# The mask of a context attention as a matmul, paced zero fills, and a planner's estimates

## The chip, the cores and the metric

The kernel runs on one core of a Trainium2 chip. The metric is the device time of one execution in microseconds (us). Times of single steps come from one profiled execution, whose span begins with the first instruction and ends with the last.

## The reference

A decoder of four layers on x of 8 x 256 tokens by 256 channels, with a context of 8 x 77 rows. Each layer has a self attention, a context attention and a feed-forward part, each followed by a residual add and a layer norm. The parts differ from layer to layer. Cut to the one that is edited, the context attention of L1 (16 heads of 64):

```python
q, k, v = heads(x @ Wq + bq), heads(ctx @ Wk + bk), heads(ctx @ Wv + bv)
scores = where(mask, -1e9, q @ k.T / 8)        # mask: 8 x 256 x 77, the same for all heads
x = layernorm(x + softmax(scores) @ v @ Wo + bo)
```

The context attention of L0 has the same sizes, without mask and biases. The feed-forward parts of L0, L1 and L2 route each token to two of 8, 8 and 14 experts.

## The kernel before, in words

**Order of the work.** The program is written batch by batch, and `Arrange` (L67 on) then reorders it. It builds the graph of all instructions, gives each an issue and a completion time (`cost`, L116 on: a formula by engine, kind and element count), adds a delay for a signal from one engine to another (`SIGNAL`, with 25 ns for pairs that are not listed), and simulates the engines. At each step an engine takes the earliest in program order among those that could start soon; it looks at most 300 instructions past the oldest one that is still open (`WINDOW`). The result is a fixed order for each of the five queues: TensorE, VectorE, ScalarE, GpSimd and SyncE, the last of which issues most DMAs. On the chip, each queue then runs strictly in that order, and an instruction that waits holds all that stand behind it on its queue. The estimates don't act on the chip; they only decide the order.

**Context attention** (`cross64`, L1308 on, for L0 and L1). Per batch of 256 tokens:
- `queries`: 8 blocks of Wq, two float32 matmuls each into PSUM, evicted to qT by VectorE and ScalarE in turn (for L1 with the bias, L570 and L572).
- `weights`: for both halves t of the tokens and both halves of the heads, 8 score matmuls (L1367) of 64 x 128 by 77 columns go into two PSUM tiles of 4 heads, 308 columns. Without a mask, VectorE takes the row maximum from PSUM (L1387) and subtracts it into P (L1388). With the mask, ScalarE first copies the scores to P in SBUF (L1380), VectorE overwrites the masked ones there with -8e9 (L1381, from mk, which SyncE loads as bytes), and maximum and subtraction then read P.
- `normed`: ScalarE takes the exponential (L1347), VectorE the sums z (L1349) and their reciprocals (L1350), and P is multiplied by them (L1351). For t = 0 it is one call of 1232 columns with the multiplication on GpSimd; for t = 1 two of 616, multiplied on GpSimd without a mask and on VectorE with it.
- `outputs`: P is transposed on TensorE (L1403), multiplied with V (L1418), and evicted to oT. Then come the output projection, the residual (GpSimd's xb, L697, then L702), and the norm: bn_stats and bn_aggr (L674, L676), an inverse root on GpSimd (L604, L605), the scaling (L685), a transpose of x (L657). Routing steps for the experts follow (L3038 to L3120), and GpSimd scatters the tokens to the experts' table l1x (L1486).

**Zero fills.** The experts' tables lie in HBM and are filled with zeros by SyncE from one SBUF tile `zero` of 128 x 256 (L1456 to L1474), which is set once in `setup` (L636). `slot_rows(kind)` issues one fill (mostly 1024 KB) per step; L0's attention makes three steps per turn of its loop for L0's and L1's tables (17 and 3 fills), and `l1_attn` (L1709 on) four per batch for L2's table, 30 fills in all. The scatter into a table waits for its fills.

**Handoff to L1's self attention.** After L0's experts, GpSimd gathers their results gy (L1530), and VectorE adds them to x (L3227), norms and hands them to the projections (L577).

Of the kernel before, what the change touches and what calls it, by code (L numbers as in the profile page):

```python
# [10 lines left out]
BF = mybir.dt.bfloat16  # L11
# [5 lines left out]
ALU = mybir.AluOpType  # L17
AX = mybir.AxisListType
# [3 lines left out]
P = 128  # L22
NB = 8
# [5 lines left out]
SC = 77  # L29
# [37 lines left out]
class Arrange:  # L67

    ENGINES = ("PE", "DVE", "Activation", "Pool", "SP")
    SIGNAL = {("DVE", "Pool"): 77, ("Activation", "Pool"): 69, ("PE", "Pool"): 100, ("DVE", "PE"): 44, ("Activation", "PE"): 43, ("Pool", "Pool"): 77}  # L70
    TABLES = [{f, "Identity", "Copy", "Square", "Relu", "Abs"} for f in ("Exp", "Ln", "Silu", "Gelu", "Gelu_apprx_tanh")]
    WINDOW, LOOK, RESERVE, SPAN = 300, 30, 2, 3413.0
    SLACK = {"PE": 100, "DVE": 150, "Activation": 200, "Pool": 200, "SP": 0}
# [42 lines left out]
    def cost(self, nd):  # L116
        i, e, kind = nd.ins, nd.e, nd.kind
        outs, ins = ([x for x in s if hasattr(x, "bass_ap")] for s in (i.outs, i.ins))
        n = max([self.count(x.ap) for x in (*outs, *ins)] or [1])
        ps = any(self.made.get(x.bass_ap.tensor.name, ("",))[0] == "ps" for x in (*outs, *ins))  # L120
        if kind == "InstMatmult":
            mv, w = ins[0], ins[1]
            n = self.count(outs[0].ap)
            wide = "float32" in str(w.dtype)
            turn = bool(i.is_transpose)
            own = n / 2.4 * (1 if not wide or turn else 4) + 3
            rows, cols = tuple(i.tile_size)
            part = 4 if 32 in (rows, cols) else 2 if 64 in (rows, cols) else 1
            low = 25 if not wide else 109 if turn else 223
            nd.pe = max(own, low), part, (rows, cols), tuple(i.tile_position), wide  # L130
            return None, nd.pe[0] + 178
        if kind == "InstDMACopy":
            on_chip = lambda x: self.made.get(x.bass_ap.tensor.name, ("dr",))[0] != "dr"
            nd.size = max([4 * self.count(x.ap) * list(x.ap)[0][1] for x in (*outs, *ins) if on_chip(x)] or [1 << 18])
            return (1250 if e == "Pool" else 60), 2000
        last = len(outs) > 1
        if e == "DVE":
            if kind in ("InstMax", "InstMaxIndex", "InstBNStatsAggregate"):
                n = 28
            elif kind == "InstReciprocal":  # L140
                n *= 5.6
            s = 65 + n / 0.96
            if n <= 256 and ps and kind == "InstTensorScalarPtr" or kind == "InstCopyPredicated":
                s += 60
            return s, s + 95
        if e == "Activation":
            if kind == "InstTensorCopy":
                s = 23 + 0.9 * n
                return s, s + 115
            s = 144 + 0.83 * n + (108 if last else 0) + (45 if not ps and 64 < n <= 512 else 0)  # L150
            return s, s + (40 if 500 < n < 600 else 105)
        if kind == "InstTensorTensor":
            s = 360 + 190 * n if n <= 8 else 145 + 2.13 * n
        elif kind == "InstMemset":
            s = 30 + 0.9 * n
        elif kind == "InstTensorCopy":
            s = 100 + 0.9 * n
        else:
            s = 240 + 0.85 * n
        return s, s + 50  # L160
# [309 lines left out]
class Build:  # L470
# [837 lines left out]
    def cross64(self, pre, bias, mask, row, route):  # L1308
        nc, a = self.nc, self.a
        with ExitStack() as ctx:  # L1310
# [9 lines left out]
                nc.sync.dma_start(kT, self.l0k[:, 6 * NC :].rearrange("p (n c) -> p n c", n=2))  # L1320
                self.l1wk = self.load_w(a["L1_xattn_Wk"], 2, 1024)
            keys = lambda n: kT[:, n, :] if bias else self.l0kT[n] if n < 6 else kT[:, n - 6, :]
            if mask is not None:
                big = self.t(w1, [P, 1], "big")
                nc.vector.memset(big, -8.0e9)
            def queries(b):

                qT = self.t(w2, [P, 8, S], "qT")
# [24 lines left out]
            def weights(b, qT):  # L1353

                Pt = []
                for t in range(2):
                    pr = self.t(w2, [P, H, SC], f"P{t}")
                    if mask is not None:
                        mk = self.t(w2, [P, SC], "mk", U8)
                        nc.sync.dma_start(mk, mask[b, t * P : (t + 1) * P, :])  # L1360
                    for hf in range(2):

                        two = [self.ps()[:, : 4 * SC].rearrange("p (h s) -> p h s", h=4) for par in range(2)]
                        for m in range(4):
                            for par in range(2):
                                r = slice(64 * par, 64 * par + 64)
                                nc.tensor.matmul(  # L1367
                                    two[par][:, m, :],
                                    qT[r, 4 * hf + m, t * P : (t + 1) * P],
                                    keys(4 * hf + m)[r, b * SC : (b + 1) * SC],  # L1370
                                    start=True,
                                    stop=True,
                                )
                        for par in range(2):
                            psv = two[par]
                            po = pr[:, 8 * hf + par : 8 * hf + 8 : 2, :]
                            mx = self.t(self.sm, [P, 4], "mx", bufs=8)
                            src = psv
                            if mask is not None:
                                nc.scalar.copy(po, psv)  # L1380
                                nc.vector.copy_predicated(  # L1381
                                    po,
                                    mk.unsqueeze(1).to_broadcast([P, 4, SC]),
                                    big.unsqueeze(1).to_broadcast([P, 4, SC]),
                                )
                                src = po
                            nc.vector.tensor_reduce(mx, src, AX.X, ALU.max)  # L1387
                            nc.vector.tensor_tensor(  # L1388
                                po, src, mx.unsqueeze(2).to_broadcast([P, 4, SC]), ALU.subtract
                            )  # L1390
# [44 lines left out]
            for b in range(NB):  # L1435
                oT = outputs(Pt, V, between)
                for _ in between:
                    pass
                if b + 1 < NB:
                    Pt = weights(b + 1, self.q_next)  # L1440
                    between = queries(b + 2) if b + 2 < NB else iter(())
                    if mask is not None:
                        for _ in range(3):
                            next(between, None)
                    V = values(b + 1)
                for t in range(2):
# [9 lines left out]
    def slot_rows(self, kind):  # L1456
# [4 lines left out]
        )[kind]  # L1461
        xg = self.t(self.dr, [n + spare, D], f"l{kind}x")
        eo = self.t(self.dr, [m, D], f"l{kind}e")
        zeroed = []
        self.slots[kind] = (xg, eo, zeroed)
        for t, first, end in ((xg, 0, n), (eo, (U0 * 256, m, U2 * 256)[kind], m)):
            for at in range(first, end, 8 * P):
                w = min(8, (end - at) // P)
                z = self.nc.sync.dma_start(
                    t[at : at + w * P, :].rearrange("(p r) c -> p r c", p=P), self.zero.unsqueeze(1).to_broadcast([P, w, D])  # L1470
                )
                if t is xg:
                    zeroed.append(z.ins)
                yield  # L1474
# [234 lines left out]
    def l1_attn(self):  # L1709
        nc, a = self.nc, self.a  # L1710
        with ExitStack() as ctx:
# [2 lines left out]
            Wqk = self.load_w(a["L1_attn_Wqk"], 2, 1024)  # L1714
            Wv = self.load_w(a["L1_attn_Wv"], 2, 256)
            Wp = self.load_w(a["L1_attn_Wp"], 2, 256)
            zeros = self.slot_rows(2)
            bk, bq = self.fm("l1_bk"), self.fm("l1_bq")
            mxps, vps = self.l1c
            rows = [slice(32 * j, 32 * j + 32) for j in range(4)]  # L1720
# [101 lines left out]
            for b in range(NB):  # L1822
# [4 lines left out]
                if b + 1 < NB:  # L1827
                    q, k, v = project_in(b + 1)
                    q2 = shift(b + 1, q, k)
                for _ in range(4):  # L1830
                    next(zeros, None)
                self.settle(1)
                weigh(*prev)
            for _ in zeros:
                pass
            self.settle()

    def heads_out(self, b, oT, W, row, pool, eps=None, route=None):
# [1612 lines left out]
```

## Time and profile before

| | |
|---|---|
| median of 3 runs | 3338.68 us (3325.26 to 3339.35) |
| the profiled execution, own time | 3340.12 us |
| its span | 3338.3 us |
| busy: TensorE, VectorE | 3038.5 us (91%), 1911.4 us (57%) |
| busy: ScalarE, GpSimd | 1080.6 us (32%), 921.4 us (28%) |
| L0's context attention | about 489 to 716 us |
| L1's self attention | about 1028 to 1335 us |
| L1's context attention | about 1334 to 1622 us |
| L1381, predicated copy x64 | 35.6 us of VectorE, 556 ns each |
| L1380, copy to SBUF x64 | 24.2 us of ScalarE |
| zero fills of L2's table | issued 1031 to 1122 us |

How to read it: PE is TensorE (PEld its weight loads), DVE VectorE, ACT ScalarE, POOL GpSimd, SP SyncE. In the slices, each digit is a fortieth of the span: the busy share in tenths, and for PEclk the clock that TensorE was granted. A group has line, engine, operation, output and inputs with their shapes, count, then busy us and mean ns of one, then the idle time just before it and what ended that. A wait has who waited, for whom, us in total, times, and the longest. A float32 matmul appears as two records.

### The profile page before, as it was taken

Reading aid. Unit: us, or ns where it says so; the run is one execution under the profiler, and the core shown is the slowest. Engines: PE = TensorE matmul, PEld = TensorE weight load, DVE = VectorE, ACT = ScalarE, POOL = GpSimd, SP = SyncE. Lnnn points to the kernel's source line nnn. Section 1 sums busy time; section 2 is a strip of 40 time slices with the busy share of each in tenths; the row PEclk is TensorE's granted clock in tenths of the full one; section 3 lists DMA queues with packets and bytes.
Section 4 is the critical chain, followed back from the end, with each engine's and each line's share of the span. In section 5 each row is a group of like instructions: output and inputs, shape, how many; then the busy total and the mean of one; then the engine's idle time right before and its main releaser. Section 6 shows DMA issues by size and latency. Waiting matters only on the chain. (4 is left out here: it accounts for less than half of the span.)

```text
span 3338.3 us, 49578 instructions
## 1 busy us (share of the span) xinstructions
PE 3038.5 (91%) x19222; PEld 2213.6 (66%) x19242; DVE 1911.4 (57%) x4814; ACT 1080.6 (32%) x2429; POOL 921.4 (28%) x1379
## 2 busy tenths in 40 slices
PE   5888779989998999899999999999898899888997
PEld 3445447758886777666555677666576588567876
DVE  6877677761003555888412132268688354699883
ACT  4666633222221223333211111145333111334441
POOL 2122253353322121223200000122244352633342
PEclk6888979999997999989999999999888899999998
DMA  4132020125547600002001133310000374200000
GB/s 161 50 100 95 26 88 25 31 84 177 186 174 249 228 14 1 23 22 78 26 4 53 42 127 129 110 44 14 1 14 26 127 234 155 83 13 4 7 7 10
DMA packets 136763, 254.04 MB, mean 76 GB/s; under 512 B 15075, under 2 KB 104939, under 8 KB 128843
## 3 DMA queue, kind: packets, MB, share of 16 engines
q1 hardware_dynamic: 112266, 150.80, 13.5%
q0 software_dynamic: 23104, 98.95, 8.7%
q8 instruction: 156, 2.56, 0.3%
q10 hardware_dynamic: 1152, 1.05, 0.1%
q14 instruction: 85, 0.69, 0.1%
HBM read 163.50 MB, written 87.26 MB: 75 GB/s over the span
## 5 line engine op out<-in xcount | busy, mean ns | idle before, releaser
L577 PE MATMUL ps<-xt,w 128*128 128x256 f32 (+1 forms) x1408 | 456.3, 471 | 3.4 <-issue 2.5
L577 PE MATMUL ps<-w,hT 128*128 128x256 f32 (+1 forms) x1792 | 399.4, 381 | 0.0
L577 PEld LDWEIGHTS ps<-w,hT 128*128 128x128 f32 (+1 forms) x1792 | 331.4, 187 | 57.4 <-issue 6.2
L577 PEld LDWEIGHTS ps<-xt,w 128*128 128x128 f32 x1408 | 266.1, 197 | 147.5 <-issue 121.3
L577 PE MATMUL ps<-gT,w 128*128 128x256 f32 (+1 forms) x1472 | 356.0, 399 | 7.3 <-ACT hT L1594 6.2
L577 PEld LDWEIGHTS ps<-gT,w 128*128 128x128 f32 x1472 | 275.1, 190 | 78.9 <-ACT hT L1594 9.7
L577 PE MATMUL ps<-w,oT 128*128 128x256 f32 x704 | 165.4, 389 | 1.0 <-ACT oT L565 0.5
L697 POOL TENSOR_TENSOR xb<-x,rows 128x256 f32<-128x256 f32 x80 | 60.0, 755 | 379.2 <-DVE res L702 379.0
L577 PEld LDWEIGHTS ps<-w,oT 128*128 128x128 f32 x704 | 133.4, 193 | 26.6 <-issue 3.8
L1594 ACT ACTIVATE hT<-ps,more 128x256 f32<-128x256 f32 x152 | 72.0, 475 | 206.2 <-PE ps L577 198.9
L1605 DVE COPY y<-ps 128x512 f32<-128x512 f32 x41 | 28.3, 691 | 172.2 <-PE ps L577 164.3
L1104 ACT ACTIVATE e<-ps,nm 128x128 bf16<-128x128 f32 (+1 forms) x256 | 104.0, 446 | 61.3 <-DVE nm L1099 60.9
L1670 DVE TENSOR_TENSOR hT<-hT,ps 128x512 f32<-128x512 f32 x56 | 38.4, 688 | 145.1 <-PE ps L577 144.2
L1403 PE MATMUL ps<-ident,P 128*77 128x128 f32 x512 | 90.8, 307 | 28.7 <-DVE P L1351 17.9
L1403 PEld LDWEIGHTS ps<-ident,P 128*77 128x77 f32 x512 | 66.6, 164 | 66.0 <-DVE P L1351 20.7
L1666 ACT ACTIVATE hT<-ps 128x512 f32<-128x512 f32 x56 | 33.3, 597 | 229.9 <-PE ps L577 229.9
L2029 DVE SCALAR_TENSOR_TENSOR f<-ps,f 128x512 f32<-128x512 f32 x128 | 80.4, 682 | 30.5 <-ACT f L2028 27.6
L1351 POOL TENSOR_TENSOR P<-P,z 128x1232 f32<-128x1232 f32 (+1 forms) x32 | 55.1, 1731 | 148.5 <-DVE z L1350 124.6
L2028 ACT ACTIVATE f<-ps,neg 128x512 f32<-128x512 f32 x128 | 78.2, 690 | 54.5 <-PE ps L2025 54.4
L1126 DVE TENSOR_REDUCE cm<-ps 128x2 f32<-128x512 f32 (+1 forms) x96 | 59.7, 684 | 53.6 <-PE ps L1067 53.3
L1418 PE MATMUL ps<-PT,V 77*64 77x256 f32 x512 | 85.1, 423 | 5.0 <-DVE PT L563 1.7
L1920 DVE TENSOR_TENSOR hT<-hT,ps 128x320 f32<-128x320 f32 x64 | 31.2, 488 | 98.3 <-PE ps L577 94.9
(669 smaller groups left out, 6467.7 us busy)
## 6 DMA issues: line engine op xcount, KB each, us to landing
l2x<-zero SPq DMA_DIRECT2D x28, 1024.0 KB
l0x<-zero SPq DMA_DIRECT2D x16, 1024.0 KB
w<-in_L_ffn_rg SPq DMA_DIRECT2D x8, 1024.0 KB
w<-in_L_ffn_ru SPq DMA_DIRECT2D x8, 1024.0 KB
w<-in_L_ffn_rd SPq DMA_DIRECT2D x8, 1024.0 KB
l2e<-y SPq DMA_DIRECT2D x22, 256.0 KB
l0e<-y SPq DMA_DIRECT2D x19, 256.0 KB
rows<-in_rows SPq DMA_DIRECT2D x7, 544.0 KB
```

What stands on the lines that cost most here:

```text
L577: self.nc.tensor.matmul(out, lhsT, rhs, start=(i == 0), stop=(i == last))
L697: self.nc.gpsimd.tensor_tensor(t, self.X[i], row, ALU.add)
L1104: nc.scalar.activation(e[:, : (t + 1) * P], ps[j][:, i, :], AF.Exp, bias=nm[:, t, h : h + 1], accum_out=z[:, t, h : h + 1],)
L1126: nc.vector.tensor_reduce(cm[:, at : at + len(gs)], ps[j], AX.X, ALU.max)
L1351: eng.tensor_tensor(pr, pr, z.unsqueeze(2).to_broadcast([P, n, SC]), ALU.mult)
L1403: nc.tensor.transpose(psv[:, m, t * P : (t + 1) * P], Pt[t][:, 2 * n + m, :], self.ident)
L1418: nc.tensor.matmul(po[64 * m : 64 * m + 64, :S], V[:, h * 64 : (h + 1) * 64], ahead[n % 2][:, m, :], start=True, stop=True,)
L1594: nc.scalar.activation(hT[:, f + m, :], ps[:, m * 256 : (m + 1) * 256], func, bias=more[:, f + m : f + m + 1])
L1666: nc.scalar.activation(hT[:, f, :], ps, func, **({"bias": bias(f)} if bias else {}))
L1670: nc.vector.tensor_tensor(hT[:, f, :], hT[:, f, :], ps, ALU.mult)
L2028: nc.scalar.activation(f[:, j], ps[j], AF.Exp, bias=neg1)
L2029: nc.vector.scalar_tensor_tensor(f[:, j], ps[j], 1.0, f[:, j], ALU.max, ALU.min)
```

## The change

1. L1's mask. GpSimd turns mk into `low` (bf16: -1e30 where masked, else 0). Before the score matmuls of a pair of PSUM tiles, TensorE multiplies the identity by `low`, repeated for four heads, into each tile, and the scores are accumulated on it. ScalarE's copy and VectorE's predicated copy go, and maximum and subtraction read PSUM.
2. Zero fills. Ahead of every second fill of L2's tables, and every third of L0's and L1's, GpSimd sets `zero` again. The memset has to wait until the fills before it have read the tile, and the next fills wait for the memset. `l1_attn` now makes two steps per batch (16), and `cross64` of L1 makes two per batch and all that are left after the last batch (14).
3. Estimates. A VectorE step that needs another VectorE step waits 50 ns instead of 25 after its completion; predicated copies and long scaled operations in SBUF (over 200 elements) complete 130 ns after issue time instead of 95; GpSimd copies 150 instead of 50; short GpSimd scalings (up to 64 elements) are estimated at 150 + 0.85 n instead of 240 + 0.85 n.

```diff
-    SIGNAL = {..., ("Pool", "Pool"): 77}
+    SIGNAL = {..., ("Pool", "Pool"): 77, ("DVE", "DVE"): 50}
...
+            if kind == "InstCopyPredicated" or kind == "InstTensorScalarPtr" and n > 200 and not ps:
+                return s, s + 130
             return s, s + 95
...
         elif kind == "InstTensorCopy":
             s = 100 + 0.9 * n
+            return s, s + 150
+        elif n <= 64 and kind == "InstTensorScalarPtr":
+            s = 150 + 0.85 * n
...
                         nc.sync.dma_start(mk, mask[b, t * P : (t + 1) * P, :])
+                        low = self.t(w2, [P, SC], "low", BF)
+                        nc.gpsimd.tensor_scalar(low, mk, -1.0e30, 0.0, ALU.mult, ALU.add)
                     for hf in range(2):
 
                         two = [self.ps()[:, : 4 * SC].rearrange("p (h s) -> p h s", h=4) for par in range(2)]
+                        if mask is not None:
+                            for par in range(2):
+                                nc.tensor.matmul(
+                                    two[par], self.identb, low.unsqueeze(1).to_broadcast([P, 4, SC]), start=True, stop=False
+                                )
...
-                                    start=True,
-                                    stop=True,
+                                    start=mask is None,
+                                    stop=mask is None or m == 3,
...
-                            src = psv
-                            if mask is not None:
-                                nc.scalar.copy(po, psv)
-                                nc.vector.copy_predicated(
...
-                                src = po
-                            nc.vector.tensor_reduce(mx, src, AX.X, ALU.max)
+                            nc.vector.tensor_reduce(mx, psv, AX.X, ALU.max)
                             nc.vector.tensor_tensor(
-                                po, src, mx.unsqueeze(2).to_broadcast([P, 4, SC]), ALU.subtract
+                                po, psv, mx.unsqueeze(2).to_broadcast([P, 4, SC]), ALU.subtract
                             )
...
+                if mask is not None:
+                    for _ in range(2 if b + 1 < NB else 30):
+                        next(self.zeros, None)
...
-        zeroed = []
+        zeroed, n_done, per = [], 0, 2 if kind == 2 else 3
...
                 w = min(8, (end - at) // P)
+                if n_done % per == 0:
+                    self.nc.gpsimd.memset(self.zero, 0.0)
+                n_done += 1
                 z = self.nc.sync.dma_start(
...
-                for _ in range(4):
-                    next(zeros, None)
+                for _ in range(2):
+                    next(self.zeros, None)
...
-            for _ in zeros:
-                pass
```

More of the change, by code (lines that the diff above doesn't have):

```diff
@@ L69 @@
     ENGINES = ("PE", "DVE", "Activation", "Pool", "SP")
-    SIGNAL = {("DVE", "Pool"): 77, ("Activation", "Pool"): 69, ("PE", "Pool"): 100, ("DVE", "PE"): 44, ("Activation", "PE"): 43, ("Pool", "Pool"): 77}
+    SIGNAL = {("DVE", "Pool"): 77, ("Activation", "Pool"): 69, ("PE", "Pool"): 100, ("DVE", "PE"): 44, ("Activation", "PE"): 43, ("Pool", "Pool"): 77, ("DVE", "DVE"): 50}
     TABLES = [{f, "Identity", "Copy", "Square", "Relu", "Abs"} for f in ("Exp", "Ln", "Silu", "Gelu", "Gelu_apprx_tanh")]
@@ L1322, in cross64 @@
             keys = lambda n: kT[:, n, :] if bias else self.l0kT[n] if n < 6 else kT[:, n - 6, :]
-            if mask is not None:
-                big = self.t(w1, [P, 1], "big")
-                nc.vector.memset(big, -8.0e9)
             def queries(b):
@@ L1377, in weights @@
                             mx = self.t(self.sm, [P, 4], "mx", bufs=8)
-                            src = psv
-                            if mask is not None:
-                                nc.scalar.copy(po, psv)
[L1381 to L1385, printed above, removed]
-                                src = po
-                            nc.vector.tensor_reduce(mx, src, AX.X, ALU.max)
+                            nc.vector.tensor_reduce(mx, psv, AX.X, ALU.max)
                             nc.vector.tensor_tensor(
-                                po, src, mx.unsqueeze(2).to_broadcast([P, 4, SC]), ALU.subtract
+                                po, psv, mx.unsqueeze(2).to_broadcast([P, 4, SC]), ALU.subtract
                             )
@@ L1716, in l1_attn @@
             Wp = self.load_w(a["L1_attn_Wp"], 2, 256)
-            zeros = self.slot_rows(2)
+            self.zeros = self.slot_rows(2)
             bk, bq = self.fm("l1_bk"), self.fm("l1_bq")
```

## The prediction, as put on record

> **What bounds the kernel now.** I read the page's slices first, then the same stretch of work in two stages, then the groups of VectorE in both, then the zero fills.
>
> ```profile
> PE   5888779989998999899999999999898899888997
> ...
> DVE  6877677761003555888412132268688354699883
> ...
> PEclk6888979999997999989999999999888899999998
> ```
>
> TensorE is busy nearly throughout, so most of the kernel is bound by it. One slice is 83.5 us. Slices 16 to 18 (1335 to 1585 us) are the L1 context attention: there VectorE stands at 8, beside 8 and 9 of TensorE. The same function runs for L0 in slices 6 and 7 without a mask. That gives a measured twin. I cut four batches out of each, from the z sum (L1349) of one batch to that of the fourth after it (busy us by engine, then granted clock, DMA share, GB/s):
>
> ```profile
> 549.36:663.24 113.88, 113.10 (x836) 88.17 (x835) 85.91 (x253) 33.48 (x68) 40.39 (x44) 1.00 0.09 31
> 1377.91:1517.36 139.45, 126.77 (x837) 96.77 (x836) 124.45 (x338) 49.94 (x116) 41.91 (x52) 0.91 0.08 25
> ```
>
> The matmul records are the same (836 and 837), yet L1 needs 139.45 us for what L0 does in 113.88. In L0 TensorE is 99% busy at full clock: it is the bound, 28.47 us a batch. In L1 VectorE is busy for 124.45 of 139.45 us, TensorE has 12.7 us of gaps and its clock falls to 0.91. VectorE, in order, is the bound there, and TensorE waits for its end of the softmax:
>
> ```profile
> PE ps L1403 <- DVE P L1351: 9.4, 4, 2.6
> ```
>
> The groups of VectorE in L1's four batches, then in L0's:
>
> ```profile
> L1388 DVE TENSOR_TENSOR P<-P,mx 128x308 f32<-128x308 f32 x33 | 21.1, 639 | 1.0
> L1381 DVE COPY_PREDICATED_SCALAR P<-mk,big 128x308 f32 x32 | 17.8, 556 | 0.0
> L1387 DVE TENSOR_REDUCE mx<-P 128x4 f32<-128x308 f32 x32 | 15.2, 474 | 1.1
> ```
> ```profile
> L1388 DVE TENSOR_TENSOR P<-ps,mx 128x308 f32<-128x308 f32 x32 | 15.1, 471 | 1.0
> L1387 DVE TENSOR_REDUCE mx<-ps 128x4 f32<-128x308 f32 x32 | 14.9, 465 | 7.1 <-PE ps L1367 7.1
> ```
>
> The maximum costs the same from PSUM (465 ns) as from SBUF (474). The subtraction is dearer from SBUF (639 against 471) because single ones are stretched while GpSimd multiplies:
>
> ```profile
> 1412.78 2.24 POOL L1351 TENSOR_TENSOR P<-P,z 128x1232 f32<-128x1232 f32 x1 [4.84 <-DVE z L1350]
> 1413.54 1.82 DVE L1388 TENSOR_TENSOR P<-P,mx 128x308 f32<-128x308 f32 x1
> ```
>
> L0 runs the same GpSimd line and never shows a subtraction over 0.48 us. The second place is the start of L1's self attention:
>
> ```profile
> L1469 SPq DMA_DIRECT2D l2x<-zero x28: 554/3010/4270, 1031.2 to 1116.6; - x28
> ```
> ```profile
> 1028.00:1058.00 30.00, 18.59 (x56) 12.15 (x54) 11.01 (x29) 5.84 (x12) 15.08 (x20) 0.67 1.00 352
> 1058.00:1100.00 42.00, 37.90 (x206) 26.41 (x208) 18.58 (x37) 6.51 (x13) 12.86 (x19) 0.72 1.05 358
> 1100.00:1140.00 40.00, 40.00 (x371) 30.81 (x367) 19.66 (x43) 13.42 (x29) 8.10 (x14) 1.00 1.01 336
> ```
> ```profile
> DVE x L3227 <- DMA gy<-l0e,rsrc: 23.5, 14, 4.6
> ...
> DVE x L3227 <- DMA gy<-l1e,rsrc: 8.8, 9, 2.8
> ...
> DVE x L3227 <- DMA gy<-l2e,rsrc: 14.6, 12, 3.6
> ```
>
> Nothing holds SyncE back, so all 30 zero fills (30 MB) go out in one burst from 1031 us, just when the L0 experts' results are gathered. VectorE waits 23.5 us for those gathers, against 8.8 and 14.6 in the two later handoffs without zeros. By 1100 us TensorE has done (busy times clock) 12.5 + 27.3 of 72 us.
>
> **The mask.** Removed per batch: 8 predicated copies of 556 ns (4.45 us of VectorE), 8 ScalarE copies of 420 ns (3.4 us; ScalarE is 36% busy, so worth nothing), and the stretched subtractions, 8 x (639 - 471) = 1.3 us. VectorE falls from 31.1 to 25.3 us a batch.
>
> Against this stands a rule. The Trainium skill, "VectorE: DVE Perf Modes", section "Rules for kernel authors", says of elementwise work on a matmul's output: take the single rate, or copy it to SBUF first if many operations follow. The kernel before obeys it and the change stops. At the page's 0.96 GHz, a double rate in SBUF would halve 308 elements from 321 to 160 ns, an estimate; losing that for two operations x 64 would cost 20 us. The rows (474 and 465, medians 479 and 478) show no double rate in SBUF, so I charge nothing.
>
> Added on TensorE: 64 matmuls of 308 columns, bf16. No such row exists here; the nearest is L1's causal mask, below after a pair that shows what a change of the tile size costs.
>
> ```profile
> 498.68 0.44 PE L1367 MATMUL ps<-w,qT 64*128 64x77 f32 x2
> 499.05 1.13 PE L577 MATMUL ps<-xt,w 128*128 128x256 f32 x4
> ...
> 1303.98 1.04 PE L1767 MATMUL ps<-causb,identb 128*128 128x512 bf16 x4
> ```
>
> The next group after L1767 starts at 1304.85: 0.87/4 = 0.217 us per 512 columns, so 0.13 for 308; 64 of them make 8.4 us. Two score records between full-size matmuls take 0.37 us to the next start, where inside a run each takes 0.058 (3.72 us for the 64 from 1338.43): two changes cost 0.25 us. The masks can cut a batch's scores into four runs instead of one: 3 x 0.25 x 8 = 6 us at most. Bounds 8.4 and 14.4; I take 11.4, 1.4 a batch.
>
> Added on GpSimd: 16 conversions of 77 columns, between L604's 0.19 us and the 0.82 us of a 768-column cast; at 0.3 us, 5 us in all, beside 30% busy. They depend only on the mask's load. If one stands behind L1351, TensorE waits up to 2.25 us, and behind it all later matmuls: 0 to 18 us for 8 batches. I take 0, since nothing of the batch is needed for it and two buffers allow it a batch early. PSUM banks are now held until the subtraction instead of 0.42 us; L0 does just that at 99% busy, so 0.
>
> New pace: 28.47 + 1.4 = 29.87 us, VectorE at 85% of it (in L0, 75%). For in-order waits at that load, and the bias and routing steps that L0 has in other form, I add 0.3: 30.15. The old pace, first to eighth z sum, is 240.2/7 = 34.31. Gain 7 x 4.15 = 29 us, and 2 in the last batch, whose 10 us at clock 0.51 (1600 to 1610) should shrink: **31 us**. What is late next is TensorE. At the first bound (masks at 8.4 us, no waits, 4 us in the last batch) it is 7 x 4.8 + 4 = 38, with 18 us of waits 13. L1's FFN behind it is bound by TensorE, so the gain passes on.
>
> The clock deserves its own look. "TensorE: Matmul & The Clock Gate", section "Why this matters for your kernels", warns only of idle gaps over about 3 us. Here no listed wait is over 2.6 us, so by the rule the clock would have been 1.00 and nothing would come back; by the row it was 0.91, some 12 of the 25.6 us between the twins. I follow the row: it is inside the 28.47.
>
> **The zero fills.** Two per batch, each pair behind a GpSimd memset of 0.31 us (L636's row): 15 memsets for L2's tables, 7 for L0's and L1's, 7 us of GpSimd. A memset waits until the pair before it has been read: 2 MB at 350 GB/s, 6 us. Behind it queue the norms' L604/L605, the scatters and the mask conversions; VectorE and TensorE wait for those. Batches are 30 us and more apart, so the wait is 0 unless the planner bunches memsets. On SyncE the mask and V loads queue behind; V has 10 us of slack (issued 1375.92, first used 1386.46). The gain: excess gather wait 23.5 - 11.7 = 11.8 us, of 32 us that TensorE lost until 1100. Bounds 3 (later collisions eat it) and 20 (the half clock goes too); I take **10**. L0's early fills: 0, at best 3.
>
> **The corrected durations** change only the planner's order, everywhere. Trace: a scaled add to its bn_stats takes 0.52 us start to start (old estimate 0.45, new 0.51), bn_stats to bn_aggr 0.46 (0.45, 0.48): better in one, worse in the other. I take 0, bounds 12 either way.
>
> **Sum.** 31 + 10 = 41 us off the profiled execution's 3340.1 (its span is 3338.3): 3299. The median of the runs is 1.4 lower: **3298**.
>
> **Rivals.** (1) TensorE goes on waiting in the L1 stage, for the conversions behind L1351 or for banks behind VectorE's queue: 18 us lost, 3340.1 - 41 + 18 - 1.4 = 3316. For it: VectorE still 85% busy; against: the twin. 22%. (2) Slower: the new order harms the stages where VectorE's chains decide, up to 460 and from 2840 us, 960 us together, where TensorE stands at 7 to 8. It decides from 41/960 = 4.3%; at 7% it is +67, so 3365. For it: the chain that ended last runs from 2840 through those very steps; against: the corrections are 25 to 100 ns on single steps. 10%, a fifth of that within 0.5%. (3) The same stages gain 2.5%, 24 us: 3274. 12%. (4) The fills stay bunched because memsets run early: 10 us less, 3308; inside the likeliest case, which has 56%.
>
> Only 0.5% (17 us) can be told from no change: 3322 and below is faster. All of the likeliest case and of (3), and four fifths of (1), lie there: 0.85. Same: a fifth of (1) and of (2), 0.07; slower 0.08. The range, 3272 to 3324, takes in (1) and (3) and leaves out (2) and the tails.
>
> **What would show it.** The z sums 30.15 us apart in L1 (34.31 would refute the mask step); TensorE's clock near 1.00 in that stage; subtractions of 0.47 us; 64 masks some 0.13 us apart. Zero fills spread from about 1065 to 1560 us, gather waits near 12 us, first projections before 1055. If the end of L1's stage is 41 us earlier but the whole isn't, the later stages' order took it. Wrong altogether if the mask conversions head TensorE's waits.

## The result, and the profile after

| | before | after |
|---|---|---|
| median, six runs each | 3336.3 us (3325.26 to 3341.5) | 3297.4 us (3293.12 to 3309.14) |
| ratio, 95% interval | | 0.9893 (0.9869 to 0.9918) |
| the profiled execution, own time / span | 3340.12 / 3338.3 us | 3293.77 / 3292.1 us |

The median fell by 38.9 us, and the profiled execution became 46.3 us shorter. Steps that both kernels have cut the span into stages, and show where:

| stage, from the start of one step to the start of the next | before | after | difference |
|---|---|---|---|
| start to the first gather of L0's results (gy<-l0e) | 1029.0 | 1033.2 | +4.2 |
| to the first score of L1's context attention (the self attention) | 309.5 | 296.7 | -12.8 |
| to its eighth z sum | 249.3 | 210.1 | -39.2 |
| to the first gather of L1's experts (gx<-l1x) | 81.2 | 79.8 | -1.4 |
| to the end of the span | 1669.3 | 1672.3 | +3.0 |

So the gain lies in two stages, the two that the edits touch, and a few us are given back outside them. The slices of the page after, one of them 82.3 us long:

```profile
PE   5888869989998999999999999999899999989997
...
DVE  6867777771113555888212232367787453688872
...
PEclk6788879999999999999999999999898999989998
```

In slices 16 to 18, counted from 0 (1317 to 1564 us), PE stands at 9, 9, 9 and its clock too, where it was 8, 9, 9 and 9, 8, 9; DVE shows 8 as before, so the gain has to be read from finer windows. Four batches of the stage, from the third z sum to the seventh (length, then busy us of PE, PEld, DVE, ACT, POOL, then clock, DMA share and GB/s), and below them three windows of the self attention:

```profile
1390.58:1509.97 119.39, 119.39 (x863) 90.14 (x862) 101.28 (x305) 39.91 (x84) 43.20 (x63) 1.00 0.32 102
1033.00:1060.00 27.00, 20.00 (x64) 14.13 (x64) 13.54 (x36) 5.83 (x12) 17.68 (x26) 0.76 0.57 194
1060.00:1100.00 40.00, 39.69 (x306) 29.38 (x305) 19.65 (x36) 10.83 (x21) 10.73 (x15) 1.00 0.33 107
1100.00:1140.00 40.00, 37.82 (x361) 27.87 (x359) 24.04 (x51) 9.46 (x20) 8.56 (x15) 0.91 0.20 67
```

The prediction's window for L1 lay one batch earlier, from the second z sum to the sixth. These are the same four batches in before:

```profile
1410.88:1553.20 142.32, 129.57 (x836) 98.74 (x835) 125.07 (x337) 49.84 (x116) 42.95 (x53) 0.89 0.08 26
```

After, TensorE is busy for all of the 119.39 us at clock 1.00; before it was busy for 129.57 of 142.32 at 0.89. VectorE went from 125.07 us to 101.28. TensorE's waits in the whole stage, the longest group of before (1338 to 1588 us) and then all of after (1330 to 1545 us):

```profile
PE ps L1403 <- DVE P L1351: 17.0, 7, 2.7
```
```profile
PE ps L1403 <- POOL P L1353: 0.4, 1, 0.4
PE ps L1403 <- DVE P L1353: 0.2, 1, 0.2
```

The three lines of the self attention are its start: the DMA share is 0.57 and 0.33 where it was 1.00 and 1.05, and from 1060 to 1100 us TensorE is busy for 39.69 of 40 us at clock 1.00, where it ran at 0.72 from 1058 to 1100. A little of that is given back from 1100 on, at 0.91. The groups of VectorE in those four batches after:

```profile
L1387 DVE TENSOR_REDUCE mx<-ps 128x4 f32<-128x308 f32 x33 | 15.5, 470 | 1.4 <-PE ps L1376 1.0 <-PE ps L582 0.4
L1388 DVE TENSOR_TENSOR P<-ps,mx 128x308 f32<-128x308 f32 x32 | 15.1, 471 | 1.0
```

The predicated copy is gone, the maximum costs what it did (470 ns), and the subtraction has come down from 639 to 471 ns. TensorE's order within a batch, at the scores:

```profile
1414.23 0.44 PE L1370 MATMUL ps<-low,identb 128*128 128x308 bf16 x2
1414.60 1.12 PE L1376 MATMUL ps<-l1kT,qT 64*128 64x77 f32 x16
1415.65 0.44 PE L1370 MATMUL ps<-low,identb 128*128 128x308 bf16 x2
```

The masks (L1370) stand in pairs between runs of 16 score records: four runs per batch, as in the prediction's upper bound. A pair takes 0.37 us to the next start. The fills, and the two waits that belong to them (who waits, for whom, us in all, times, longest):

```profile
L1475 SPq DMA_DIRECT2D l2x<-zero x28: 512/606/863, 1055.7 to 1465.0; - x28
```
```profile
DVE x L3231 <- DMA gy<-l0e,rsrc: 12.5, 11, 3.2
...
POOL zero L1473 <- DMA l2x<-zero: 7.6, 1, 7.6
```

The 28 large fills, issued within 85 us before, are spread over 409 us. VectorE's wait for the gathers fell from 23.5 to 12.5 us. One memset of 22 waited 7.6 us on a fill, until 1265.0 us. No mask conversion stood behind it (the first starts at 1327.9 us), and neither memsets nor conversions stand among TensorE's waits.

### The profile page after: what moved, and what is told of

The parts are those of the page before. It is cut to its first block, busy times and chain, and to the rows that moved or that the text cites. A ratio compares the mean times of both kernels' runs of the same rounds, so it can differ in the third digit from the quotient of the medians.

```text
span 3292.1 us, 49716 instructions
## 1 busy us (share of the span) xinstructions
PE 3042.4 (92%) x19306; PEld 2214.8 (67%) x19306; DVE 1856.1 (56%) x4749; ACT 1057.0 (32%) x2365; POOL 932.6 (28%) x1417
## 3 DMA queue, kind: packets, MB, share of 16 engines
q10 hardware_dynamic: 1152, 1.05, 0.1%
## 5 line engine op out<-in xcount | busy, mean ns | idle before, releaser
L582 PE MATMUL ps<-xt,w 128*128 128x256 f32 (+1 forms) x1408 | 443.3, 462 | 4.7 <-issue 3.8
L1349 ACT ACTIVATE P<-P 128x616 f32<-128x616 f32 (+1 forms) x48 | 42.6, 888 | 144.6 <-DVE P L1388 120.8
L1561 DVE COPY gT<-ps 128x512 f32<-128x512 f32 x19 | 13.1, 692 | 127.7 <-PE ps L1554 113.7
L610 POOL TENSOR_TENSOR rs<-rs,mhalf 128x1 f32<-128x1 f32 x144 | 80.7, 560 | 12.0
L1418 PE MATMUL ps<-PT,V 77*64 77x256 f32 x512 | 82.3, 409 | 1.1 <-issue 0.9
```

What stands on the lines that cost most here:

```text
L582: self.nc.tensor.matmul(out, lhsT, rhs, start=(i == 0), stop=(i == last))
L610: self.nc.gpsimd.tensor_tensor(out, out, self.mhalf[: in_.shape[0], :w], ALU.pow)
L1349: nc.scalar.activation(pr, pr, AF.Exp, scale=0.125)
L1418: nc.tensor.matmul(po[64 * m : 64 * m + 64, :S], V[:, h * 64 : (h + 1) * 64], ahead[n % 2][:, m, :], start=True, stop=True,)
```

## The experiments

The theory is that of the prediction: in the stage before, VectorE's order set the pace, the change takes work off it until TensorE binds, and the zero fills' collision with the gathers is worth some 10 us beside it. Against it stand three rivals: the planner's new order brings the time, not the edits; TensorE still waits for VectorE after the change; and what pays is not the smaller VectorE work but the way that the scores travel (through ScalarE and SBUF before, straight from PSUM now). The runs come in three groups, each on a chip of its own. The chips differ (before took 3315.9, 3339.8 and 3338.8 us on them), so a kernel's whole time is compared as its ratio to before on the same chip, and stages are read from the traces. The ratio with its interval is not the quotient of the medians in the tables; the two can differ by some 7 us (e1_mask: 18 us by the ratio, 25 between the medians).

Some measures recur. "Score to z8" is the time from the first score of L1's context attention to its eighth z sum. "Pace" is the mean of the six periods from the second z sum to the eighth (seven periods, as in the prediction, take in a first batch that behaves otherwise). "TensorE's work" is its busy time multiplied by its clock in four batches, per batch; the clock has two digits, so that is good to some 0.15 us.

**Each part alone.** The first group takes the change apart. Its diffs are the parts of the diff shown above: e1_mask is before with part 1 only, e2_fills with part 2 only, e3_estimates with part 3 only, e4_mask_fills with parts 1 and 2.

> The kernel before with the mask on TensorE alone; fills and estimates stay as they were. My theory (VectorE bound the L1 context attention, TensorE binds it now): the z sums are 30.0 us apart instead of 34.3, the stage is 36 to 38 us shorter, and the whole is 31 to 38 us faster (ratio 0.989 to 0.991). Rival (the gain of the full change comes as much from the estimates that order that stage): the z sums stay at 32 us or more and the whole gains under 20 us.

> The kernel before with the paced zero fills alone. My theory: the start of L1's self attention gains 10 to 16 us (between the first gather of L0's results and the second batch's scores), and the whole is 8 to 14 us faster, since the fills that now fall into the context attention cost nothing there. Rival (paced fills only move the collisions to later batches): the whole gains under 4 us.

> The kernel before with the corrected estimates alone. In the profile of the full change the first scatter of L0 is 5.4 us later than before, and from the gather of L2's results to the end 4 us are lost. Theory: the new order causes both, so this kernel is 5 to 10 us slower than before. Rival (the memsets of the L0 fills cause the first, chance the second): within 3 us of before.

> The full change without the corrected estimates. If parts add up, and the estimates cost what the profile of the full change suggests: 45 to 52 us faster than before, so 5 to 10 us faster than the full change (39 us). Rival (the estimates are neutral or help): 36 to 42 us faster than before.

| | median us | ratio to before, 95% interval | first gather to first score | score to z8 |
|---|---|---|---|---|
| e1_mask | 3291.0 | 0.9945 (0.9923 to 0.9967) | 293.3 | 211.1 |
| e2_fills | 3306.9 | 0.9978 (0.9962 to 0.9995) | 286.3 | 250.0 |
| e3_estimates | 3322.5 | 1.0026 (1.0011 to 1.0042) | 297.0 | 238.3 |
| e4_mask_fills | 3280.7 | 0.9905 (0.9885 to 0.9926) | 289.1 | 211.1 |

Each edit acts in its own stage. With the mask on TensorE, score to z8 is 211.1 us, with or without the fills, against 250.0 with the fills alone. With the fills paced, the self attention takes 286.3 and 289.1 us, against 293.3 and 297.0 without: 4 to 11 us, and 4.2 between e1 and e4, which differ in the fills alone. The chip probably matters here: with the fills in one burst the stage takes 309.5 us in the first profile of before and 310.1 in b1_before. The estimates alone make the kernel slower, by 0.26% (8.6 us by the ratio, 6.6 between the medians). Yet they shorten score to z8 by 11.7 us (238.3 against e2's 250.0): the new order is better where VectorE binds, and loses more than that in other stages. That gain doesn't add to the mask's, since with the mask on TensorE the stage takes 210.1 us with the estimates (the full change) and 211.1 without. The rival that the order brings the time is out: mask and fills without it reach the ratio of the whole change.

Two expectations on the whole time were missed. The mask alone was to bring 31 to 38 us and brought 18 to 25, though its stage is 38.9 us shorter than in e2; mask and fills were to bring at least 36 and brought 31 to 35. In the profiles, e1 stands 7.0 us behind e2 in the self attention, where e2 has the paced fills, and 8.4 behind L1's context attention (1676.3 against 1667.9 us). What costs those 8.4 us wasn't tried.

**What binds after.** The second group ran the two kernels again (b1_before, in a single run, and a1_full, the whole change) beside two edits of the whole change. e5_two_masks adds each mask a second time, which costs TensorE work and nobody else:

```diff
+                                nc.tensor.matmul(
+                                    two[par], self.identb, low.unsqueeze(1).to_broadcast([P, 4, SC]), start=False, stop=False
+                                )
```

> The kernel before, once more, for a profile on the chip of the runs that it is compared with. Theory: the L1 context attention lasts 331 us from its first score to the first load of the experts' rows, as in the first profile and in the kernel with paced fills alone.

> The full change once more, to place it against the mask and fills without the estimates (35 us or 0.9905 of before). If the corrected estimates cost 5 to 8 us as they do alone: 27 to 30 us faster than before, ratio 0.991 to 0.992. If they only harm the old order and not the changed kernel: ratio 0.989 to 0.9905.

> The full change with every mask matmul issued twice (each masked score gets -2e30). If TensorE binds the stage now, as I hold, each doubled matmul is paid in full: 64 x 0.13 us = 8.4 us slower than the full change, z sums 31.1 us apart instead of 30.0. Rival (VectorE's queue at 85% still sets the pace): under 3 us slower, z sums under 30.4 apart.

The third group has its counterpart, e7_no_mask: the mask is left out of the computation, so that TensorE multiplies no mask and GpSimd converts none.

```diff
-                        low = self.t(w2, [P, SC], "low", BF)
-                        nc.gpsimd.tensor_scalar(low, mk, -1.0e30, 0.0, ALU.mult, ALU.add)
...
-                                nc.tensor.matmul(
-                                    two[par], self.identb, low.unsqueeze(1).to_broadcast([P, 4, SC]), start=True, stop=False
-                                )
...
-                                    start=mask is None,
-                                    stop=mask is None or m == 3,
+                                    start=True,
+                                    stop=True,
```

> The full change with the mask left out altogether (no masked scores; mk is loaded and not used). If TensorE binds the stage, the 64 mask matmuls and the array's changes of shape are what it saves: z sums 28.5 to 28.7 us apart, 9 to 12 us faster than the full change. Rival (VectorE's load or the conversions on GpSimd hold the pace): z sums stay above 29.5.

Four batches of a1_full, then of e5_two_masks, then of e7_no_mask:

```profile
1393.01:1513.03 120.02, 120.02 (x866) 90.71 (x865) 101.40 (x306) 39.97 (x84) 43.55 (x64) 1.00 0.32 102
```
```profile
1391.39:1516.41 125.02, 125.02 (x897) 93.46 (x897) 101.03 (x306) 39.76 (x84) 46.24 (x65) 1.00 0.32 102
```
```profile
1383.71:1496.65 112.94, 112.94 (x834) 89.03 (x833) 101.42 (x304) 38.99 (x84) 41.38 (x57) 1.00 0.33 106
```

In all three, TensorE is busy for the whole window at clock 1.00. With 32 more matmuls in four batches the window grows by 5.00 us (0.156 us each), with 32 fewer it shrinks by 7.08, while VectorE stays at 101 us. So TensorE binds after the change, and takes what is laid on it in full; the rival of a TensorE that still waits is out. Score to z8 goes 199.8, 210.1, 218.8 us for no, one and two masks. By e7, the mask costs 7.08/4 = 1.77 us a batch, of which 8 x 0.156 = 1.25 is the matmuls by e5; the remaining 0.52 us is what the second mask doesn't pay again. The starts in the traces put it at the changes between masks and scores. In a batch of after, the four pairs take 1.47 us to the next start and the scores, in four runs, 4.20; in e7 the scores take 3.89, in a run of 4 records (0.38) and this one of 60:

```profile
1405.25 3.58 PE L1369 MATMUL ps<-l1kT,qT 64*128 64x77 f32 x60
1408.76 2.86 PE L582 MATMUL ps<-xt,w 128*128 128x256 f32 x12
```

1.47 + 4.20 - 3.89 = 1.78 us, the mask's cost again. On the whole time, e5 gives 0.9915 (0.9895 to 0.9935) beside a1_full's 0.9890 (0.9867 to 0.9912), and e7 0.9865 (0.9851 to 0.9879): in the same order, but with intervals that overlap between neighbours.

**What made the old pace.** Three kernels stand between the two. e6_scores_in_sbuf keeps the mask on TensorE, but ScalarE copies the masked scores to SBUF, and maximum and subtraction read them there, as they did before:

```diff
-                            nc.vector.tensor_reduce(mx, psv, AX.X, ALU.max)
+                            src = psv
+                            if mask is not None:
+                                nc.scalar.copy(po, psv)
+                                src = po
+                            nc.vector.tensor_reduce(mx, src, AX.X, ALU.max)
...
-                                po, psv, mx.unsqueeze(2).to_broadcast([P, 4, SC]), ALU.subtract
+                                po, src, mx.unsqueeze(2).to_broadcast([P, 4, SC]), ALU.subtract
```

> The full change, but ScalarE copies the masked scores from PSUM to P first, and maximum and subtraction read P, as before. Tells the predicated copy from the stretched subtraction. If TensorE binds: VectorE goes from 25.3 to 26.6 us a batch, still below 30, so 0 to 3 us slower than the full change, with subtractions of 0.64 us on the mean. Rival (the removed double read of SBUF was what paid): 8 to 12 us slower, z sums over 31 apart.

It came out at 3336.93 us, 0.9982 (0.9971 to 0.9994): nearly the whole gain is gone, 29 us above a1_full, though the predicated copy is off VectorE. That was against the theory, and beyond the 8 to 12 us of its rival. Its four batches, two groups in them, and three waits:

```profile
1396.50:1530.41 133.91, 124.76 (x866) 92.30 (x865) 107.78 (x304) 51.07 (x117) 45.23 (x65) 0.97 0.30 96
```
```profile
L1392 DVE TENSOR_TENSOR P<-P,mx 128x308 f32<-128x308 f32 x32 | 21.2, 664 | 1.0
L1391 DVE TENSOR_REDUCE mx<-P 128x4 f32<-128x308 f32 x32 | 15.0, 467 | 2.6 <-ACT P L1389 2.6
```
```profile
PE ps L662 <- DVE x L690: 6.3, 4, 1.6
...
DVE PT L568 <- PE ps L1407: 10.0, 8, 2.9
DVE z L1351 <- ACT P L1349: 5.3, 4, 1.3
```

VectorE is busy for 107.78 us, where b1_before had 124.57 of 136.90 in the same batches, yet the window is only 3 us shorter. No engine is full: TensorE is busy for 93% at clock 0.97, VectorE for 80%, ScalarE for 38%. VectorE waits for TensorE's transposes and for ScalarE's copies and exponentials, TensorE for the norm of VectorE, and the subtraction is stretched again (664 ns). What is left is the chain through three engines that each run in order; that it sets the pace is inferred, from no engine being full and from what e9 and a1_full gain by shortening it.

e9_copy_for_max then splits the two uses: the copy stays, but only the maximum reads it, and the subtraction reads PSUM.

```diff
-                            nc.vector.tensor_reduce(mx, psv, AX.X, ALU.max)
+                            src = psv
+                            if mask is not None:
+                                src = po
+                                nc.scalar.copy(po, psv)
+                            nc.vector.tensor_reduce(mx, src, AX.X, ALU.max)
```

> The full change, but ScalarE copies the scores to P and only the maximum reads that copy; the subtraction reads PSUM and overwrites P. Against the kernel with both in SBUF (29 us slower than the full change) this leaves the detour over ScalarE and takes the second SBUF input of the subtraction away. If stretched subtractions were the cause: subtractions of 0.47 us, z sums 30 to 30.5 apart, under 5 us slower than the full change. If the detour is (one more engine in the chain of each half, in ScalarE's order): z sums 32 or more, 18 us or more slower.

e10_predicated_in_psum goes the other way: VectorE's predicated copy stays, but works on the scores in PSUM; no mask on TensorE, no copy by ScalarE. Of its edit, the lines on VectorE; the mask's lines go as in e7.

```diff
...
+                                nc.vector.copy_predicated(
+                                    psv,
+                                    mk.unsqueeze(1).to_broadcast([P, 4, SC]),
+                                    big.unsqueeze(1).to_broadcast([P, 4, SC]),
+                                )
                             nc.vector.tensor_reduce(mx, psv, AX.X, ALU.max)
...
```

> The full change with the mask taken off TensorE: VectorE's predicated copy writes -8e9 into the scores in PSUM, then maximum and subtraction read PSUM, with no detour over ScalarE. VectorE has 25.3 + 4.5 = 29.8 us of work a batch, TensorE 28.5. If the predicated copy's time was what bound the old stage, as my prediction had it: VectorE binds near 31 to 32 us a batch, 10 to 16 us slower than the full change. If the detour was: z sums 29 to 30 us apart, within 5 us of the full change.

The groups of e9 in its four batches, and then those of e10 with its window:

```profile
L1392 DVE TENSOR_TENSOR P<-ps,mx 128x308 f32<-128x308 f32 x32 | 15.1, 471 | 2.9
L1391 DVE TENSOR_REDUCE mx<-P 128x4 f32<-128x308 f32 x32 | 14.9, 466 | 1.6 <-ACT P L1390 1.6
```
```profile
L1384 DVE COPY_PREDICATED_SCALAR ps<-mk,big 128x308 f32 x32 | 15.6, 534 | 0.0
L1390 DVE TENSOR_TENSOR P<-ps,mx 128x308 f32<-128x308 f32 x32 | 15.1, 471 | 1.0
```
```profile
1394.79:1519.55 124.76, 118.02 (x834) 88.96 (x833) 114.41 (x336) 38.86 (x84) 41.26 (x56) 0.99 0.28 94
```

In e9 the subtraction, from PSUM, is back at 471 ns with the copy still there. A subtraction beside GpSimd's multiplication in e6, and the same pair in e9:

```profile
1398.37 2.28 POOL L1353 TENSOR_TENSOR P<-P,z 128x1232 f32<-128x1232 f32 x1 [3.46 <-DVE z L1352]
...
1398.96 2.02 DVE L1392 TENSOR_TENSOR P<-P,mx 128x308 f32<-128x308 f32 x1
```
```profile
1394.93 2.25 POOL L1353 TENSOR_TENSOR P<-P,z 128x1232 f32<-128x1232 f32 x1 [3.28 <-DVE z L1352]
...
1395.60 0.48 DVE L1392 TENSOR_TENSOR P<-ps,mx 128x308 f32<-128x308 f32 x1
```

So the stretch belongs to reading SBUF beside that multiplication. As a whole, e9 lies between its two answers: a pace of 31.41 us, and 0.9935 against the full change's 0.9890. In e10 VectorE is at 92% of the window and TensorE at 95%.

| | mask by | scores read from | median us | ratio, 95% interval | score to z8 | pace | TensorE's work a batch |
|---|---|---|---|---|---|---|---|
| b1_before | VectorE | SBUF | 3344.3 (one run) | | 245.2 | 34.25 | 29.1 |
| e6 | TensorE | SBUF | 3336.9 | 0.9982 (0.9971 to 0.9994) | 232.9 | 33.23 | 30.3 |
| e9 | TensorE | SBUF by the maximum only | 3315.2 | 0.9935 (0.9921 to 0.9949) | 219.4 | 31.41 | 30.3 |
| a1_full | TensorE | PSUM | 3307.9 | 0.9890 (0.9867 to 0.9912) | 210.1 | 30.12 | 30.0 |
| e10 | VectorE | PSUM | 3314.0 | 0.9918 (0.9903 to 0.9933) | 226.1 | 31.07 | 29.2 |

The 35 us of score to z8 from b1_before to a1_full fall apart, in the table's order, into 12.2 for taking the predicated copy off VectorE, 13.5 for the subtraction from PSUM, and 9.3 for dropping ScalarE's copy. In the other order, 19.1 are for reading PSUM at once with no copy, and 16.0 for the mask on TensorE. So about half is the mask's new engine and half the scores' new way, and only with both is the pace that of TensorE's work. Two executions of before differ by 4 us in this stage (249.3 and 245.2), so the shares are no finer than that. And the planner orders each of these kernels anew; e3 shows that order alone can move the stage by 11.7 us, so a share is that of a step together with its order, and no run here separates the two.

**Later fills.** e8_late_fills keeps all fills out of the first three batches of the self attention, and makes three per batch in the context attention.

```diff
-                    for _ in range(2 if b + 1 < NB else 30):
+                    for _ in range(3 if b + 1 < NB else 30):
...
-                for _ in range(2):
+                for _ in range(2 if b > 2 else 0):
                     next(self.zeros, None)
```

> The full change with no zero fill in the first three batches of L1's self attention (2 in each of the other five, then 3 per batch in the context attention). If the first pairs still collide with the gathers of L0's results (12.5 us of waits, TensorE's clock at 0.66 from 1130 to 1140 us): gather waits near 9 us and 3 to 6 us faster than the full change. Rival (one pair per batch is hidden): within 2 us.

The waits for the gathers fell further, from 12.5 to 8.7 us:

```profile
DVE x L3231 <- DMA gy<-l0e,rsrc: 8.7, 10, 1.8
```

The stage from first gather to first score took 294.1 us against a1_full's 297.6, but the whole is where it was: 0.9893 (0.9879 to 0.9908). The two ran on different chips, so the 3.5 us are not counted. Between these two placings of paced fills no difference shows, and no version here is shown to beat the change.

## Why the prediction was right, point by point

It said 3298 us, and the median was 3297.4. That nearness is partly luck: the mask's stage and the fills gained more than the sum had, outside them 7 us were lost that it had put at 0, and the median of before came out at 3336.3 with six runs, where the sum started from 3338.68.

**What binds.** Right for the kernel after: TensorE, at clock 1.00 and fully busy, with VectorE at 85% of the window (101.28/119.39), the very share that was forecast. e5 and e7 show it by the price of added and removed matmuls. For the kernel before it is half right. TensorE did wait for VectorE's P, but VectorE's load was not all that set the pace: in e6 it fell from 91% to 80% of the window, and the pace only from 34.25 to 33.23 us. The way of the scores over ScalarE and SBUF made up the rest.

**The base of 28.47 and the 0.3 for waits.** e7 without a mask has 28.24 a batch, against 28.47 + 0.3 = 28.77 in the sum. The L0 twin was a good measure, and no wait had to be added at all.

**The mask's cost on TensorE.** Mis-sized: 1.4 us a batch was taken, 1.77 measured, just under the upper bound of 14.4/8 = 1.8. One matmul took 0.156 us instead of 0.13 (1.25 us a batch instead of 1.05), all four runs per batch did occur, and the changes cost 0.52 us a batch, where 0.75 was the most and half of it was taken. The base, 0.5 us lower than the sum had it, made up for it: the last six periods average 30.12 us, where 30.15 was the forecast.

**The gain of 31 us in the stage.** 40.6 us measured (39.2 + 1.4), 37.0 by b1_before and a1_full. The last six periods brought 29.2 us ((34.98 - 30.12) x 6) and in that second pair of profiles 24.8 ((34.25 - 30.12) x 6), against 6 x 4.15 = 24.9 in the sum. The old pace of 34.31 was a mean with the first period of 30.35 in it; the six behind it average 34.98. What the sum left out is the start: the first period shrank from 30.35 to 23.28 us, 7.1 instead of 4.15, and the time from the first score to the first z sum from 9.1 to 6.1. Why the first batch gains more isn't tried. In the tail, the stretch at half clock became shorter but is not gone; before, then after:

```profile
1600.11:1613.77 13.66, 13.29 (x52) 8.41 (x53) 9.06 (x33) 3.82 (x11) 2.76 (x5) 0.50 0.00 1
```
```profile
1554.35:1561.18 6.83, 6.83 (x26) 3.87 (x23) 4.32 (x22) 1.53 (x4) 0.00 (x0) 0.50 0.00 0
```

The time from the eighth z sum to the first gather of L1's experts fell by 1.4 us; the sum had 2, so the term most mis-sized is the first batch.

**"ScalarE is 36% busy, so worth nothing."** This step failed, without harm to the total. Dropping ScalarE's copy was worth 9.3 us between e9 and a1_full, though ScalarE's busy share is as low as forecast. The copy is a link in the chain from scores to maximum, and VectorE waits behind it in order. In the same way, reading PSUM was worth more than the stretch in the rows: 8 x (664 - 471) = 1.5 us of VectorE a batch, but 1.82 of pace between e6 and e9. The total still came out since the sum was made from the pace of a twin that has neither copy nor stretch, not by adding the removed steps.

**The rule on copying to SBUF.** The Trainium skill, "VectorE: DVE Perf Modes", section "Rules for kernel authors", offers the copy to SBUF when many operations follow. I charged nothing for leaving it; the runs go further. With the maximum at 467 ns from SBUF and 470 from PSUM, and the subtraction dearer from SBUF where it meets GpSimd's multiplication, the copy bought nothing here; with both operations behind it, it cost 29 us (e6 against a1_full).

**The clock.** The Trainium skill, "TensorE: Matmul & The Clock Gate", section "Why this matters for your kernels", names gaps over about 3 us. The row was followed, and it held: with the short waits gone, the clock went from 0.91 (0.89 in the later window) to 1.00. In e6's four batches no listed wait of TensorE is over 1.6 us, and its clock is 0.97. In the tail of after it was 0.50 for 6.83 us, though the longest idle time of TensorE in the 14 us before that was 0.75 us; in e7, with 0.85 and 0.69 us in the same place, it stayed at 1.00. So the runs give no length of wait at which the clock falls.

**The fills.** 10 us forecast for them; the self attention became 12.8 us shorter, 12.6 between b1_before and a1_full, and 4 to 11 us in the group of the single parts. Gather waits of 12.5 us were forecast as near 12. First projections started at 1056.1 us, not before 1055, though the first gather came 4.2 us later than before. The fills ran from 1055.7 to 1465 us; the forecast had 1065 to 1560. Only one memset waited long for a fill, 7.6 us, near the 6 of the forecast, and TensorE didn't wait for it.

**The estimates, at 0.** Inside their bound of 12, but not nothing: alone they cost 0.26% (0.11 to 0.42), some 7 to 9 us. In the profiles of all kernels with the new order, L2's attention and its neighbours, from the first gy<-l1e to the first gy<-l2e, took 705.7 us on average (nine profiles, 691.9 to 712.3), with the old order 696.7 (five, 691.8 to 701.0); the two ranges overlap, and the profiles come from several chips. Whether they cost the full change as much isn't settled: e4_mask_fills without them has 0.9905, a1_full with them 0.9890, the intervals overlap, and the two didn't run on the same chip.

**L0's start, at 0 to -3.** It went the other way: L0's first scatter came at 545.4 us, 5.4 later than in before. With the old order and no memsets it lay at 540.0 to 544.2, with either or both at 543.2 to 548.3. Whether the memsets of L0's fills or the new order delay it is left open.

**The rivals.** (1) fell by e5 and e7. (2) and (3), the new order, act by less than the 67 and 24 us they were given: L2's part is 9 us longer on average, and L1's context attention 12 us shorter only where VectorE binds. (4) fell by the fills' row.

## What to carry to other kernels

When one engine's order holds up another that is nearly full, price the change from a twin stage without the step, and check the new bound's added work; a sum over the removed steps misses what the chain between engines costs. A copy by an idle engine isn't free if a later step waits for it in order: ask for its place in the chain, not for the busy share. And a planner's order that helps where an engine binds may help nothing once the bound has moved: e3's 11.7 us in the stage were gone when the mask lay on TensorE.

## What the runs showed of the hardware that was not expected

- The subtraction of 308 float32 columns from SBUF took up to 1.82 us in before and 2.03 in e6 where it ran beside GpSimd's multiplication of 1232 columns, and most others took 0.48 us; from PSUM none took over 0.48 us, with the same GpSimd work beside it (e9).
- The predicated copy took 534 ns on PSUM and 556 on SBUF: on PSUM it needs no detour.
- The clock varies between executions of one program, and moves the time of a stage as much as an edit. L2's attention in two profiles of the full change:

```profile
2102.50:2582.50 480.00, 445.67 (x3618) 303.62 (x3617) 357.33 (x989) 180.09 (x347) 166.43 (x262) 0.92 0.09 30
```
```profile
2105.90:2599.10 493.20, 461.33 (x3617) 314.39 (x3616) 355.13 (x989) 180.36 (x347) 166.33 (x261) 0.89 0.09 30
```

TensorE's busy time times its clock is some 410 us in both; the stretch takes 480.0 us at 0.92 and 493.2 at 0.89. Differences of some 10 us between single executions say little; a stage where TensorE is full at clock 1.00 repeats within 0.1 us (score to z8 210.1, 210.1 and 210.1 us in after, a1_full and e8).
